# The order of a feed-forward kernel's opening: byte stores on other queues, earlier fetches, and a written order of loads and stores in its first stage

## The chip, the cores and the metric

The kernel runs on one core of a Trainium2 chip. The time is that of the device for one execution, in microseconds; before the change the median of three runs was 2055.12 us (2054.68 to 2055.93).

Five engines work side by side, each through its own instructions in order: TensorE (PE: matrix products and transposes into PSUM), VectorE (DVE), ScalarE (ACT), GpSimd (POOL) and SyncE (SP, which here only issues DMAs). ACT and POOL can issue DMAs too. Engines wait for each other by semaphores. An instruction that waits holds back all that stand behind it on its engine.

## The reference

The input is u, 2 x 1024 rows of 1024 values. Three blocks are added to it in turn: half a feed-forward block, a state-space convolution (S4), and half the same feed-forward block again.

```python
x = L0_attn_u
x = x + 0.5 * ffn(layernorm(x))
x = x + s4(layernorm(x))
x = x + 0.5 * ffn(layernorm(x))

def ffn(x):
    Wg, Wu, Wd = dequant(gate), dequant(up), dequant(down)
    h = silu(x @ Wg) * (x @ Wu)
    return h @ Wd

# W[k, n] = scales[k // 128, n] * (w4[k, n] - (z4[k // 128, n] + 1))
```

The weights are 4-bit numbers, eight to a 32-bit word, with a scale and a zero point for every 128 rows of a column. Gate and up have 1024 rows and 2752 columns, down has 2752 rows and 1024 columns.

## The kernel before, in words

The 2048 rows are taken in four blocks of 512. Each passes the feed-forward block twice, so there are eight jobs (j = 0 to 7). Each job has a gate and up stage and then a down stage.

**The gate and up stage** (`gate_up`) runs over 64 steps. A step is a wave w (three, and in the last three waves two, column blocks of 128 of gate and as many of up) and a group g of 128 rows of the weights, g = 0 to 7. In each step every unit (one block of gate or up; a wave of three has six) gets two products of 128 x 128 by 128 x 512: the normalized input is split into xTh (about the upper part of each number) and xTl (the rest), and both are multiplied by the same whole-number weights (L803). A unit has one PSUM bank. After both products of a group the bank is multiplied in place by the ratio of two groups' scales (`scaled`: L766 on ACT or L770 on DVE), so that the sums of all groups add up in the bank. I call that an eviction, though the values stay in the bank. Units of gate go to ACT, units of up to DVE, with exceptions for the second unit of a wave (L816): in job 0 it goes to ACT at g = 0 and g = 4. After the last group, ACT takes the Silu of gate (L831), DVE multiplies with up (L834), and POOL splits the result in two (L836, L838). Only then are the two banks free for the next wave. There are eight banks, and six are held by a wave of three.

**The weights.** For each step a tile of bytes is loaded by SP from `w_q[w]` in HBM four steps ahead (`load_bytes`, L727), and three steps ahead it is cast to 32-bit numbers (`make_weights`), by POOL (L743), or by ACT in job 0 where s mod 8 is 1, 2 or 5 (L741). The bytes in `w_q` are made in job 0 itself. Wave by wave, the packed words are fetched (`fetch`, L556), the unpacked zero points are fetched from `z_dram`, spread over 16 rows each (`fetch_zeros`, L563), DVE turns the words into two sets of bytes (`split` with `signed_bytes`: mask L617, add L619, sign L621, for the even and the odd nibbles), POOL copies out each of the eight nibble positions (`dequantize`, L650), and SP stores them to `w_q` (L651). So in job 0 the load for a wave's step has to wait for all eight stores of that wave. `first_weights` says at which step each piece is placed: words and zeros of wave w + 1 three steps into wave w's own schedule, and so on.

**The opening** (`start`) does the same for wave 0 by `first_split`: its words come from SP and ACT, DVE makes the bytes, POOL copies out nibbles 1, 3, 5, 7, 4 and 6 (L601) and ACT 0 and 2 (L599). Each copy is stored twice: 16 of its 128 rows into the first weight tile in SBUF (L602, SP), and all of it to `w_q[0]` (L604; by SP for 0 and 2, by POOL for the others). Meanwhile x is loaded and its mean and variance are found (`first_moments`: DVE for rows 0 and 2, ACT for 1 and 3), the deviation's inverse r is found by an integer guess (L203 to L209) and three refinements (L224 to L228), and the rows are normalized (`first_rows`, by DVE for even t in the first half, else by ACT). PE transposes them in chunks of 128 columns (`first_turn`, L1751); ACT copies the result to xTh (L1753) and DVE subtracts for xTl (L1754). `keep_warm` gives PE transposes whose results nobody uses. The zero points are unpacked by DVE (L355, L364) and stored to `z_dram` by SP (L383). The scales of wave 0 are loaded and turned, copied by DVE (L426), inverted and made into ratios (L392 to L432). Chunks 0 and 1 are turned in `start`, chunks 2 to 7 in steps 0 to 5.

**What sets the order.** The code places pieces at steps as hooks: `at(up, s, f)` runs f before the matmuls of step s, and at s + 0.5 after half of them. But the tile framework may reorder instructions of an engine by its own estimate of times. `in_order_of_writing(f, engines)` (and `pinned`, which wraps it) forbids that: each instruction that f writes for one of these engines is bound to come after the one written before it. `STARTING` is ACT, DVE and SP; `start` is pinned on these and PE.

## Time and profile before

| what | value |
|---|---|
| median of 3 runs | 2055.12 us (2054.68 to 2055.93) |
| the profiled execution | 2054.89 us |
| its span in the trace | 2053.0 us |
| granted TensorE clock, mean | 0.998 |
| first matmul with weights (L803) | 22.46 us |
| end of job 0's gate and up stage | about 200 us |
| PE busy | 2007.7 us (98%) |
| DMA, share of 16 engines, main queue | 35.0% |

How to read it: times are counted from the start of the span. A row of a timeline gives start, length, engine, line of the code, operation, and the tiles (output <- input); "x3" joins three like instructions, and brackets give the idle time before and who ended it. An engine's name with q (SPq, ACTq) is its queue of DMA issues. In a view of stretches, each engine has its busy time and the number of instructions in it (an instruction across an edge counts on both sides), and the last three columns are the granted clock of PE, the share of the DMA engines in use and GB/s; columns of engines without such instructions are left out. PEld is the load of weights into PE, which runs beside the matmuls. Matmul lengths are modelled, so gaps and starts say more than busy time. A wait is put down to whoever came last by the profile.

### The profile page before, as it was taken

How to read it: one execution, taken by the hardware profiler on the slowest of the kernel's cores; microseconds unless marked ns; L12 is line 12 of the kernel's file. 1: busy time of each engine (PE TensorE's matmuls, PEld its weight loads, DVE VectorE, ACT ScalarE, POOL GpSimd, SP SyncE). 2: the span in 40 equal slices, each digit the busy share in tenths (PEclk: the TensorE clock that was granted, in tenths of full speed). 3: DMA queues.
4: the chain of work that ended last, by engine and by line, in shares of the span. 5: the costliest groups of instructions: out<-in, count | busy, mean ns of one | idle time of the engine just before them, and what ended most of it. 6: DMA issues, size and time to landing. Idle time of an engine off the chain costs nothing.

```text
span 2053.0 us, 29946 instructions
## 1 busy us (share of the span) xinstructions
PE 2007.7 (98%) x9204; PEld 1371.8 (67%) x9204; DVE 1653.2 (81%) x2836; ACT 1409.5 (69%) x2208; POOL 1353.4 (66%) x1742
## 2 busy tenths in 40 slices
PE   6999999999999999999999999999999999999998
PEld 4555775577766678665876578667686576866576
DVE  8888878867888787878778777887878878777776
ACT  6777787747675476777767777664776647767775
POOL 5867768657865478755976568753686646965542
PEclk9999999999999999999999999999999999999999
DMA  4434332243623227411462126333163331661113
GB/s 142 124 89 146 115 87 78 60 78 99 166 79 85 88 49 187 146 32 35 121 183 81 31 51 164 87 83 90 40 158 104 71 92 41 156 189 42 34 35 102
DMA packets 346887, 197.15 MB, mean 96 GB/s; under 512 B 168069, under 2 KB 324590, under 8 KB 346718
## 3 DMA queue, kind: packets, MB, share of 16 engines
q1 hardware_dynamic: 345414, 192.74, 35.0%
q8 instruction: 75, 1.23, 0.2%
q10 hardware_dynamic: 1016, 1.82, 0.2%
q14 instruction: 94, 0.77, 0.1%
q0 software_dynamic: 288, 0.59, 0.1%
HBM read 127.52 MB, written 48.57 MB: 86 GB/s over the span
## 4 chain that ended last, share of the span: by engine, by line
PE 91%; DVE 3%; POOL 2%; DMA 1%; issue 1%; ACT 1%; SPq 0%; ACTq 0%; POOLq 0%; DVEq 0%
PE pg L803 56%; PE po L877 30%; PE pc L1245 3%; PE pb L1245 1%; DVE pg L770 1%; DMA b<-wq 1%; POOL hh L836 0%; POOL w_up L743 0%; ACT pg L766 0%; POOL hl L838 0%; DMA x<-in_L_attn_u_dram 0%; POOL q L650 0%; POOL sums L1239 0%; DMA st<-sz 0%; DVE hf L834 0%
## 5 line engine op out<-in xcount | busy, mean ns | idle before, releaser
L766 ACT ACTIVATE pg<-pg,rat 128x512 f32<-128x512 f32 x1270 | 801.6, 661 | 398.6 <-PE pg L803 394.7
L770 DVE TENSOR_TENSOR pg<-pg,rat 128x512 f32<-128x512 f32 x1138 | 755.1, 692 | 142.9 <-PE pg L803 135.2
L803 PE MATMUL pg<-xTh,w_up 128*128 128x512 f32 x2752 | 851.1, 437 | 2.8 <-DVE pg L770 1.9
L803 PE MATMUL pg<-xTl,w_up 128*128 128x512 f16 x2752 | 715.8, 382 | 9.2 <-DVE pg L770 3.8
L743 POOL CAST w_up<-b 128x768 fp32r<-128x768 int8 (+2 forms) x490 | 376.4, 775 | 396.8 <-PE pg L803 286.6
L803 PEld LDWEIGHTS pg<-xTh,w_up 128*128 128x128 f32 x2752 | 519.2, 189 | 170.5 <-issue 10.4
L766 ACT ACTIVATE po<-po,ratd 128x512 f32<-128x512 f32 x669 | 438.0, 662 | 144.0 <-PE po L877 143.1
L877 PE MATMUL po<-hl,w_down 128*128 128x512 f32 x1344 | 526.4, 393 | 2.5 <-DVE po L770 1.3
L877 PE MATMUL po<-hh,w_down 128*128 128x512 f32 x1344 | 521.4, 390 | 0.0
L770 DVE TENSOR_TENSOR po<-po,ratd 128x512 f32<-128x512 f32 x611 | 423.8, 696 | 112.0 <-PE po L877 111.3
L803 PEld LDWEIGHTS <-w_up 128*128 128x128 bf16 x2752 | 226.8, 98 | 347.8 <-issue 164.3
L743 POOL CAST w_down<-bd 128x512 fp32r<-128x512 int8 x352 | 218.6, 625 | 152.0 <-PE po L877 75.9
L877 PEld LDWEIGHTS po<-hl,w_down 128*128 128x128 f32 x1344 | 251.9, 188 | 64.9 <-DVE po L770 4.4
L877 PEld LDWEIGHTS po<-hh,w_down 128*128 128x128 f32 x1344 | 252.4, 188 | 50.8
L838 POOL TENSOR_TENSOR hl<-hf,hh 128x512 fp32r<-128x512 f32 x168 | 218.7, 1302 | 7.1
L836 POOL CAST hh<-hf 128x512 fp32r<-128x512 f32 x168 | 108.0, 643 | 76.2 <-DVE hf L834 46.2
L834 DVE SCALAR_TENSOR_TENSOR hf<-pg,rat,g 128x512 f32<-128x512 f32 x168 | 120.9, 746 | 40.7 <-ACT g L831 30.6
L831 ACT ACTIVATE g<-pg,rat 128x512 f32<-128x512 f32 x168 | 110.1, 687 | 34.9 <-PE pg L803 18.2
L930 POOL TENSOR_TENSOR x<-x,yr 128x512 f32<-128x512 f32 x52 | 67.0, 1288 | 0.0
L295 POOL TENSOR_TENSOR lo<-x,hi 128x512 f16<-128x512 f32 x48 | 62.5, 1301 | 0.0
L189 DVE BATCH_NORM_STATS2 stats<-x 128x6 f32<-128x512 f32 x88 | 59.9, 681 | 0.0
L293 POOL TENSOR_TENSOR mid<-hi,top 128x512 bf16<-128x512 f32 x48 | 56.2, 1171 | 0.0
(214 smaller groups left out, 1083.6 us busy)
## 6 DMA issues: line engine op xcount, KB each, us to landing
b<-wq SPq DMA_DIRECT2D x319, 96.0 KB
bd<-wdq SPq DMA_DIRECT2D x336, 64.0 KB
x<-in_L_attn_u_dram SPq DMA_DIRECT2D x30, 512.0 KB
yz<-y SPq DMA_DIRECT2D x56, 256.0 KB
yr<-yz SPq DMA_DIRECT2D x56, 256.0 KB
b<-wq SPq DMA_DIRECT2D x128, 64.0 KB
sz<-xn SPq DMA_DIRECT2D x16, 512.0 KB
st<-sz SPq DMA_DIRECT2D x64, 128.0 KB
```

The costliest lines, as they stand in the source:

```text
L295: nc.gpsimd.tensor_tensor(lo[:, own], n[:, own], hi[:, own].bitcast(F32), ALU.subtract)
L743: nc.gpsimd.tensor_copy(t, b)
L766: nc.scalar.activation(dst, src, AF.Copy, scale=sc)
L770: nc.vector.tensor_tensor(dst, src, sc.to_broadcast(list(dst.shape)), ALU.mult)
L803: nc.tensor.matmul(p, weights, (lo, hi)[k][:, g, :], start=(g == 0 and not done), stop=(g == GK - 1 and done), skip_group_check=True,)
L831: nc.scalar.activation(g, pg, AF.Silu, scale=rat[:, 2 * f, GK - 1 :])
L834: nc.vector.scalar_tensor_tensor(hf, pu, last, g, ALU.mult, ALU.mult)
L836: nc.gpsimd.tensor_copy(hi, hf)
L838: nc.gpsimd.tensor_tensor(lo, hf, hi.bitcast(F32), ALU.subtract)
L877: nc.tensor.matmul(ps[c], w[:, bass.ts(c, P)], part, start=(f == 0 and k == 0), stop=(f == NF - 1), skip_group_check=True,)
L930: nc.gpsimd.tensor_tensor(part, part, rows_back.pop((a, t)), ALU.add)
L1245: nc.tensor.matmul(dst, lhsT, rhs, start=start, stop=stop, skip_group_check=True)
```

## The change

- **Byte stores of wave 0.** `first_split` gets a function `keep`, so that storing to `w_q[0]` is separate from copying out. Nibbles 1, 3, 5, 7 are stored by SP, 4 and 6 by POOL after all its copies, 0 and 2 by ACT.
- **Wave 1's words** are fetched before the moments of x are taken, and no longer after all copies.
- **Zero points.** The eight unpacking instructions go between the moments and the guess; the last one follows the second group of rows; the store to `z_dram` and the fetch of wave 1's zeros are placed at step 0, pinned on SP. Wave 2's words and zeros follow at steps 1 and 2.
- **Scales of wave 0.** Turned after four warming transposes, copied by ACT instead of DVE; the inverse is written between xTh and xTl of chunk 0. The rows of scales for blocks 3 to 8 are loaded at step 1 instead of in `start`.
- **Rows and chunks.** The order of the row pieces in `start` changes; the second halves of rows 0 and 2 go from ACT to POOL; chunks 1 and 2 come in the middle of step 0, chunk 3 at step 1, chunk 4 in the middle of step 2; they are pinned on PE too, and chunks 2 and 3 on POOL. The second halves of rows 1 and 3 come at steps 0.5 and 1, pinned on ACT.
- **Matmuls and evictions.** In job 0 the matmuls of steps 0 to 5 are pinned on PE, step 0's evictions on ACT and DVE. In job 0 the second unit of a wave goes to ACT only at g = 4.
- **Loads and stores.** In job 0, `next_weights` is pinned on SP for steps below 52. `dequantize` no longer stores; `keep_bytes` does, at steps of its own, pinned on SP. The copies of wave 1 are all placed at step 3.
- **Within a split** both masks come first, then add and sign of each half.

The diff, cut to its core:

```diff
@@ -379,6 +379,7 @@
         yield from unpacked_zeros_in_pieces(tab, z, zi)
+        yield
         dst, seg = (zd_dram, SEGD) if which else (z_dram, SEG)
         nc.sync.dma_start(dst.rearrange("g (s n) -> (g s) n", s=seg), tab)
@@ -408,7 +409,10 @@
     def scales(k0, k1, rows):
-
+        for _ in scales_in_pieces(k0, k1, rows, nc.vector.tensor_copy):
+            pass
+
+    def scales_in_pieces(k0, k1, rows, copy):
...
-        nc.vector.tensor_copy(flat(s), ps[:, : (u1 - u0) * GK])
+        copy(flat(s), ps[:, : (u1 - u0) * GK])
+        yield
         inv = t2(f"inv_{k0}")[:, : (u1 - u0) * GK]
         inverse(inv, flat(s), k0)
@@ -600,10 +605,13 @@
             nc.sync.dma_start(first_tile[j:P:8], q[: P // 8])
-            queue = nc.sync if j in (0, 2) else nc.gpsimd
-            queue.dma_start(w_q[0].rearrange("(r j) n -> j r n", j=8)[j], q)
-
-        return rest, dequantize
+            bytes_of[j] = q
+
+        def keep(j, queue):
+            queue.dma_start(w_q[0].rearrange("(r j) n -> j r n", j=8)[j], bytes_of.pop(j))
+
+        bytes_of = {}
+        return rest, dequantize, keep
@@ -613,9 +621,10 @@
         for part, (n, shift) in zip((even, raw), shifts):
+            nc.vector.tensor_scalar(part, raw, n, NIBBLES, shift, ALU.bitwise_and)
+            yield
+        for part in (even, raw):
             both = part.bitcast(U16)
-            nc.vector.tensor_scalar(part, raw, n, NIBBLES, shift, ALU.bitwise_and)
-            yield
             nc.vector.tensor_tensor(both, both, z.bitcast(U16), ALU.add)
             yield
             nc.vector.tensor_scalar(both, both, 0x8080, None, ALU.bitwise_xor)
@@ -648,9 +657,14 @@
         nc.gpsimd.tensor_copy(q, packed[w][j % 2][:, j // 2, :])
-        nc.sync.dma_start(w_q[w].rearrange("(r j) n -> j r n", j=8)[j], q)
+        ready[w, j] = q
         if j == 7:
             packed.pop(w)
+
+    ready = {}
+
+    def keep_bytes(w, j):
+        nc.sync.dma_start(w_q[w].rearrange("(r j) n -> j r n", j=8)[j], ready.pop((w, j)))
@@ -688,14 +702,19 @@
         for w in range(1, len(WAVES)):
             s0 = (0, 4, 8 * w - 15)[min(w, 3) - 1]
-            steps = (0, 1, 2, 2, 3, 3) if w == 1 else range(6)
+            steps = (0.5, 1, 2, 2.5, 2.5, 3) if w == 1 else range(6)
             in_pieces(at, [(up, s0 + d) for d in steps], lambda w=w: split(w))
-            copies = {1: (2, 2, 3, 3, 3, 3, 3, 3), 2: (3, 3, 4, 4, 6, 6, 7, 7)}
+            copies = {1: (3,) * 8, 2: (3, 3, 4, 4, 6, 6, 7, 7)}
+            copies = copies.get(w, (3, 3, 4, 5, 6, 6, 7, 8))
+            stores = {1: (3,) * 8, 2: (4.5, 4.5, 5.5, 5.5, 7, 7, 7.5, 7.5)}
+            stores = stores.get(w, [d + 1.5 for d in copies])
             if 1 < w < len(WAVES) - 1:
                 both = lambda w=w: (fetch(w + 1), fetch_zeros(w + 1))
                 at(up, s0 + 3, lambda both=both: in_order_of_writing(both, ET.SP))
-            for k, d in zip((0, 2, 4, 6, 1, 3, 5, 7), copies.get(w, (3, 3, 4, 5, 6, 6, 7, 8))):
+            for k, d, o in zip((0, 2, 4, 6, 1, 3, 5, 7), copies, stores):
                 at(up, s0 + d, lambda w=w, k=k: dequantize(w, k))
+                store = lambda w=w, k=k: keep_bytes(w, k)
+                at(up, s0 + o, lambda store=store: in_order_of_writing(store, ET.SP))
@@ -773,7 +792,7 @@
         for s, (wi, g) in enumerate(STEPS):
-            w = next_weights()
+            w = in_order_of_writing(next_weights, *[ET.SP] * (j == 0 and s < 52))
             for hook in hooks.get(s, ()):
                 hook()
@@ -800,7 +819,7 @@
-                nc.tensor.matmul(
...
+                in_order_of_writing(product, *[ET.PE] * (j == 0 and s < 6))
                 if not done:
                     continue
                 if g < GK - 1:
                     on_act = unit % 2 == 0
                     if unit == 2 * fs[0] + 1:
-                        on_act = (j == 0 and g % 4 == 0) or (j == 1 and g % 2 == 0)
+                        on_act = (j == 0 and g == 4) or (j == 1 and g % 2 == 0)
                         on_act = on_act or (j in (3, 4) and 24 < s < 33)
                     if unit == 2 * WIDE:
                         on_act = g % 2 == 0
-                    scaled(on_act, p, p, rat[:, unit, g : g + 1])
+                    rescale = lambda: scaled(on_act, p, p, rat[:, unit, g : g + 1])
+                    in_order_of_writing(rescale, *STARTING[:2] * (j == s == 0))
@@ -1612,20 +1633,24 @@
             if j == 0:
-                rows = {3: srow_next}
-                for first_use, s, k0, k1 in ((5, 0, 3, 9), (14, 6, 9, 15), (30, 11, 15, WIDE)):
-                    if k0 > 3:
-                        load = lambda k0=k0, k1=k1: rows.update({k0: scale_rows(k0, k1)})
-                        at(up, s, lambda load=load: in_order_of_writing(load, ET.SP))
+                rows = {}
+                for s, f in ((0, lambda: next(points, None)), (0, lambda: fetch_zeros(1)), (1, lambda: fetch(2)), (2, lambda: fetch_zeros(2))):
+                    at(up, s, pinned(f, ET.SP))
+                for first_use, s, k0, k1 in ((5, 1, 3, 9), (14, 6, 9, 15), (30, 11, 15, WIDE)):
+                    load = lambda k0=k0, k1=k1: rows.update({k0: scale_rows(k0, k1)})
+                    at(up, s, lambda load=load: in_order_of_writing(load, ET.SP))
                     at(up, first_use, lambda k0=k0, k1=k1: scales(k0, k1, rows.pop(k0)))
                 at(up, 36, lambda: rows.update(down=scale_rows_down()))
...
-                for c in range(2, NC):
+                for c in range(1, NC):
                     more = lambda c=c: rows_by_chunk(c)
-                    at(up, c - 2, lambda more=more: in_order_of_writing(more, *STARTING))
+                    at(up, {1: 0.5, 2: 0.5, 4: 2.5}.get(c, c - 2), pinned(more, *STARTING, ET.PE, *[ET.Pool] * (1 < c < 4)))
+                for i, t in enumerate((1, 3)):
+                    more = lambda t=t: first_rows(t, 512, HID)
+                    at(up, 0.5 + i / 2, pinned(more, ET.Activation))
@@ -1732,12 +1757,13 @@
-        if t % 2 or half:
+        if t % 2:
             nc.scalar.activation(n, src, AF.Identity, bias=first["bias"][:, t : t + 1], scale=r)
         else:
-            nc.vector.tensor_scalar(n, src, m, r, ALU.subtract, ALU.mult)
-
-    def first_turn(c):
+            e = nc.gpsimd if half else nc.vector
+            e.tensor_scalar(n, src, m, r, ALU.subtract, ALU.mult)
+
+    def first_turn(c, between=lambda: None):
...
         if c != 5:
             nc.scalar.copy(hi, ps)
+            between()
             nc.vector.tensor_tensor(lo, ps, hi.bitcast(F32), ALU.subtract)
     def rows_by_chunk(c):
-        if c < 4:
+        if 1 < c < 4:
             first_rows(2 * c - 4, 512, HID)
         first_turn(c)
@@ -1781,38 +1808,41 @@
-        rest, dequantize_first = first_split(zq)
-        for j in (1, 3, 5, 7):
-            dequantize_first(j)
-        mv, scratch = first_moments({0: rest, 2: lambda: None})
+        rest, dequantize_first, keep_first = first_split(zq)
+        for pair in ((1, 3), (5, 7)):
+            for j in pair:
+                dequantize_first(j)
+            for j in pair:
+                keep_first(j, nc.sync)
+        fetch(1)
+        points = zero_points_in_pieces(0, zeros)
+        mv, scratch = first_moments({0: rest, 2: lambda: [next(points) for _ in range(8)]})
         for j in (4, 6, 0, 2):
             dequantize_first(j)
-        fetch(1)
-        rows_next = scale_rows(3, 9)
-        keep_warm(22, scratch)
+        for j in (4, 6):
+            keep_first(j, nc.gpsimd)
+        keep_warm(4, scratch)
+        first_scales = scales_in_pieces(0, 3, srow, nc.scalar.copy)
+        next(first_scales)
+        for j in (0, 2):
+            keep_first(j, nc.scalar)
+        keep_warm(12, scratch)
         bias = small.tile([P, NT], F32, tag="bias", name="bias")
         r = deviations(0, 1, LIFT)
         nc.vector.scalar_tensor_tensor(bias, mv[:, :, 0], -1.0, r, ALU.mult, ALU.mult)
         first["bias"] = bias
         for t in range(NT):
             first_rows(t, 0, P)
-        zero_points(0, zeros)
-        for t in (0, 2):
+        for t in (0, 1):
             first_rows(t, P, 512)
-        first_turn(0)
-        for t in (1, 3):
+        first_turn(0, lambda: next(first_scales, None))
+        for t in (2, 3):
             first_rows(t, P, 512)
+        next(points)
         keep_warm(6)
-        scales(0, 3, srow)
-        first_turn(1)
-        for t in (1, 3):
-            first_rows(t, 512, HID)
-        fetch_zeros(1)
-        fetch(2)
-        fetch_zeros(2)
-        return rows_next, zeros_down
-
-    srow_next, zeros_down = in_order_of_writing(start, *STARTING, ET.PE)
+        return points, zeros_down
+
+    points, zeros_down = in_order_of_writing(start, *STARTING, ET.PE)
```

More of the change, by code (lines that the diff above doesn't have):

```diff
@@ L615, in signed_bytes @@
         for part, (n, shift) in zip((even, raw), shifts):
-            both = part.bitcast(U16)
             nc.vector.tensor_scalar(part, raw, n, NIBBLES, shift, ALU.bitwise_and)
             yield
+        for part in (even, raw):
+            both = part.bitcast(U16)
             nc.vector.tensor_tensor(both, both, z.bitcast(U16), ALU.add)
@@ L802, in gate_up @@
                     weights = weights.bitcast(BF16).rearrange("p (n k) -> p k n", k=2)[:, 1, :]
-                nc.tensor.matmul(
+                product = lambda: nc.tensor.matmul(
                     p,
```

## The prediction

> **What bounds the kernel now.** I read the page first, then TensorE's (PE's) matmuls by stretch, then what PE waits for, then the timeline of the first 25 us and the chain of waits where it stalls longest.
>
> The page's first part and its clock row:
>
> ```profile
> PE 2007.7 (98%) x9204; PEld 1371.8 (67%) x9204; DVE 1653.2 (81%) x2836; ACT 1409.5 (69%) x2208; POOL 1353.4 (66%) x1742
> ...
> PEclk9999999999999999999999999999999999999999
> ```
>
> PE is the bound, so a microsecond by which its first matmul comes earlier, or a gap that closes, should come off the end. The change touches only the start and the first gate and up stage (j = 0). That stage in three stretches, matmuls of L803 alone (length, busy and count):
>
> ```profile
> 22.40:83.05 60.65, 50.91 (x204) 26.80 (x205) 0.97 0.44 127
> 83.05:147.90 64.85, 62.99 (x278) 37.47 (x277) 1.00 0.31 90
> ```
>
> PE's steady pitch is read from a stretch without gaps: 144 instructions in 32.35 us (83.05 to 115.40), 0.225 us each. At it the first 204 need 45.9 us; 24 transposes of x after the first matmul (0.11 us each in the timeline) add 2.6 and 15 of scales 1.0. So 49.5 us would do where 60.65 passed: 11.1 us are lost, after 22.46 us before the first matmul. From 83.05 on hardly anything is lost (DVE waits of 2.7 us in all up to 205). Who held PE, 0 to 205 us (total, times, longest):
>
> ```profile
> PE pg L803 <- DVE pg L770: 3.5, 9, 0.8
> PE pg L803 <- ACT g L831: 3.1, 1, 3.1
> PE pg L803 <- POOL w_up L743: 1.7, 2, 1.2
> PE pt L1751 <- DVE xn L1738: 1.4, 2, 0.8
> PE pt L1751 <- DVE xTl L1754: 1.2, 1, 1.2
> ```
>
> The opening, from the timeline (start, length):
>
> ```profile
> 14.19 2.14 DVE L207 TENSOR_SCALAR half<-ve 128x4 int32<-128x4 int32 x1
> ...
> 14.71 1.60 POOL L601 COPY q<-even_w 128x768 int8<-128x768 int8 x2
> ...
> 18.18 0.50 SPq L602 DMA_DIRECT2D b<-q  x1
> ...
> 20.21 1.00 POOL L743 CAST w_up<-b 128x768 fp32r<-128x768 int8 x1 [2.90 <-DMA b<-q]
> ```
>
> Two chains meet at the first matmul: the bytes (last store into the first weight tile issued by 18.68, landed 1.53 later, cast to 21.2), and the normalization (r known at 18.50 because one 128x4 instruction took 2.14 us, then rows, transposes, xTh and xTl to 22.4). The longest stall, from the chain of waits:
>
> ```profile
> 70.80 0.30 SPq L563
> ...
> 72.27 4.19 DMA b<-wq
> ...
> 77.28 0.83 ACT w_up L741
> 78.10 0.59 ACT g L831
> ...
> 78.74 11.32 PE pg L803 x42
> ```
>
> SP issued the loads of the fifth wave's words and zeros (L563) ahead of a weight tile's load, which took 4.19 us to land beside them. ACT stood 3.35 us in front of the cast of that tile, and the Silus that free PE's banks stood behind it. PE was idle from 75.65 to 78.74. It pays twice:
>
> ```profile
> 78.80:82.30 3.50, 3.50 (x9) 1.99 (x9) 2.13 (x3) 2.83 (x5) 3.08 (x5) 0.51 0.33 111
> ```
>
> After the gap the granted clock was 0.51 for 3.5 us, so 1.75 more was lost.
>
> **Part by part.** *The start, bytes.* Six stores of wave 0 went from POOL (0.54 to 0.73 us each, between its casts) and two from SP. Now SP takes j = 1, 3, 5, 7, POOL 4 and 6 after all its casts, ACT 0 and 2. SP's queue, from its rows (tile store 0.50, byte store 0.58, fetch 0.43): two tile stores after the casts at 10.12 and 10.9, to 11.40; two byte stores to 12.55; again two and two to 14.70; wave 1's fetch, two DMAs, to 15.55; four tile stores to 17.55, instead of 18.68. Landed 1.53 later, at 19.1; cast by 20.1. The Trainium skill speaks against moving stores (DMA: Bandwidth & Descriptors, Rules for kernel authors): spreading DMAs over SP, ACT and GpSimd brings no bandwidth, for all share the same engines, and saves the issuing engine's time only. The rows agree on the price, since the DMA share is 0.26 from 10 to 20 us. By the rule alone the edit is worth nothing on the wire; by the rows issue time is just what this chain is made of, so I count 1.1 us.
>
> *The start, normalization.* Eight zero-unpacking instructions (0.83 us) leave the place after the rows and go to 12.77, where DVE waits 0.92 us for ACT's squares; ztab (0.52) goes behind xTl. The casts of j = 4 and 6 no longer wait for POOL's stores (2 x 1.07 and 1.28 us between pairs), so the six end near 14.1 and not at 16.3. That matters for L207: such a 128x4 instruction takes 0.17 (L209), and it took 2.14, ending 0.03 after POOL's casts. The Trainium skill (SBUF — State Buffer, Who interferes with whom) says why: DVE's two-port forms and GpSimd share one port pair under an exclusive lock, and the later one blocks fully. By the row, L207 at 14.19 finds POOL done and r is ready at 16.5 (L209 ran its 0.17 under a POOL store). By the rule the unpacking, now beside POOL's casts, may itself block to 14.1 and push everything behind it: r at 17.75. Neither end is excluded; I take 17.3, gain 1.2. From r: rows 0.9 on ACT, a further row piece 0.66 (now ahead of xTh), xTh 0.59, xTl 0.68; on DVE the inverse of the scales (1.3, now between) is done by 19.8. So xTl is ready near 20.5, and the weights near 20.1: first matmul 20.5, gain 2.0 (0.6 to 2.6). The scale copy (0.25) and two stores (about 0.6 each) on ACT lie in its idle 3.43 us before the rows; warm-up falls from 22 to 16 transposes plus 3, and the clock is already full.
>
> *Steps 0 to 7.* Before, ACT did three half-row normalizations (2.23) before it evicted step 0's banks. Now two go to POOL, two come later, step 0's evictions are held in written order, and PE's first six steps too. POOL pays two 128x512 instructions: nearest rows, cast 0.62 and two-input subtract 1.29; it reads one tensor, so about 0.8 each, and they lie in the 5.94 us that POOL stood idle before 33.55. g = 0 of the second unit moves from ACT to DVE, +0.63 us (three in 1.88) per wave on DVE. By dependences, step 1 starts 3.7 us after step 0 (six matmuls 1.35, ACT two evictions and xTh 1.9 more, xTl), not 4.75. Later steps lose less to ACT and to the wait for a bank; DVE is 93% busy here (14.04 of 15.10 us, 36.5 to 51.6), which limits it. Of the 6.0 us lost outside the long stall I take half, 3.0 (from -1.5 to +5).
>
> *SP's fixed order.* Weight loads up to step 51 now stand before the same step's fetches and stores, and byte stores come 1 to 1.5 steps after their copies. Queued behind a waiting store are only later steps' loads, 4 steps (11 us) ahead of use. The tile that landed late would be issued as soon as wave 2's bytes are home, about 68, and not behind five other DMAs. The 3.5 us between matmuls and the 1.75 of clock should go: 5.0 with a small rest. Next late is the last byte store of wave 1: raw bytes from about 32, POOL then has 8 copies (6.6), chunk 5 (2.6) and a cast (0.8) and ends near 39.5; store, load and cast (1.9 + 2.4 + 0.8) give 44.7, while step 8 starts near 48. Cover about 3 us. Wave 1's zeros are written after ztab, near 23, and fetched by 26.5, while DVE needs them near 28.
>
> *Later waves.* DVE gets 0.63 us more in each of five waves, at 86% load (94.64 of 110 us from 90 to 200). ACT is relieved by as much just when it has three Silus. Between -3.3 and +1 I take -0.8, since DVE waits showed in the last four waves alone. The extra yields and the changed order within the split cost nothing: same instructions.
>
> **Sum.** 2.0 + 3.0 + 5.0 - 0.8 = 9.2 us. The profiled execution took 2054.89 (span 2053.0 and 1.9 around it): 2045.7. The median of 2055.12 is 0.23 above it: 2045.9, say 2046.
>
> **The rivals.**
> - *The stall moves on* (0.25): the long wait goes, but POOL's copies or DVE's evictions hold PE for several short ones, so the middle term is 0 and DVE costs 2: 2.0 + 5.0 - 2 = 5, 2050. For it: DVE's 93%, and POOL instructions drawn out to 1.55 us beside DVE's. Against: POOL idle 7.3 us for late weight bytes, which now come earlier.
> - *Only the start gains* (0.10): another dependence sets SP's order (wave 2's bytes are home at 68 anyway), and the tile still meets the fetches on the wire. 2.0, and 2053. Against: the chain shows SP's own issues directly ahead of the late load.
> - *Slower* (0.06): the order holds SP at the head. Eight stores of wave 1 stand at step 3 ahead of step 8's load. If POOL's last copy ends after 43 us rather than 39.5, each us is idle PE, and from about 3 us of idleness the clock halves as it did at 78.7. Five us plus 1.7 at step 8, and the same at step 16, is 13.4 against 9.2: 2059.
> - *The forecast* (0.59): 2046, own range 2042 to 2049.
>
> Within 0.2% (4.1 us) is about what a measurement of this kernel can't tell from no change. Faster by more takes the forecast and over nine tenths of the first rival, 0.83; same 0.11; slower 0.06. The range, 2042 to 2051.5, leaves out the slower case, most of the third, and the upper ends of start and steps together.
>
> **What would show it.** First matmul near 20.5 and L207 near 0.2 us; if L207 is still long or the unpacking takes over 1 us, the lock went the other way. The 204th matmul near 73 rather than 83. No ACT wait for b of over 1 us near 70, and clock 1.00 from 75 to 85. SP's loads ahead of the fetches; the last store of wave 1 near 40. DVE waits after 83 at most 4 us. I am wrong if PE still has a gap of 3 us before 85, or if the stage after 83 (116.8 us now) grows by more than 3.

## The result, and the profile after

The changed kernel took 2052.48 us (median of 22 runs, 2051.34 to 2056.78) against 2055.65 (22 runs) before: a ratio of 0.9986, interval 0.9979 to 0.9992. The gain is real, 3.2 us (1.6 to 4.3), a third of the 9.2 forecast, and the time lies above the range. The profiled execution has a span of 2050.5 us. Its page:

```profile
PE 2006.6 (98%) x9198; PEld 1371.1 (67%) x9198; DVE 1655.4 (81%) x2843; ACT 1403.3 (68%) x2199; POOL 1351.8 (66%) x1740
...
PEclk9999999999999999999999999999999999999999
```

The averages hardly move; what moved is seen when the products with weights are counted (12 in a step of waves 0 to 2) and the start of the n-th is compared, in us:

| product | before | after | difference | forecast for this stretch | measured |
|---|---|---|---|---|---|
| 1st | 22.46 | 20.69 | -1.77 | -2.0 | -1.77 |
| 181st (step 15) | 72.78 | 71.91 | -0.87 | -3.0 | +0.90 |
| 205th (step 17) | 83.07 | 79.65 | -3.42 | -5.0 | -2.55 |
| 688th (end of the stage) | 199.27 | 194.93 | -4.34 | +0.8 | -0.92 |

The sum at the 688th is 4.3, and the spans differ by 2.5; the rest of the program gives some back, and the difference of the medians, 3.2, lies between the two. The matmuls by stretch, as before (length, busy and count, clock):

```profile
20.60:79.60 59.00, 50.23 (x204) 1.00 0.44 125
79.60:144.45 64.85, 63.05 (x280) 1.00 0.33 94
```

The first stretch holds the same 204 products and is only 1.65 us shorter, about as much as the clock alone had cost (1.75); what the long stall and the start released was used up by other gaps. The second row was given the same length as before, so the length says nothing; counted by products, the 205th to the 481st took 64.51 us against 64.76, so VectorE's extra evictions cost nothing there. Who held PE from 0 to 205 us (total, times, longest):

```profile
PE pg L822 <- DVE pg L789: 6.1, 8, 1.5
PE pg L822 <- POOL w_up L762: 1.4, 1, 1.4
PE pg L822 <- ACT g L852: 1.3, 1, 1.3
```

The wait of 3.1 us for ScalarE's Silu became 1.3, and VectorE's evictions took its place: 6.1 us instead of 3.5. That is the rival "the stall moves on" (2050), worked further than it was priced.

The opening, from the timeline:

```profile
12.26 2.10 DVE L355 TENSOR_SCALAR zi<-zq 128x43 int32<-128x43 int32 x8
...
14.75 0.17 DVE L207 TENSOR_SCALAR half<-ve 128x4 int32<-128x4 int32 x1
...
15.53 2.40 SPq L607 DMA_DIRECT2D b<-q  x4
...
19.30 0.69 DVE L1781 TENSOR_TENSOR xTl<-pt,xTh 128x512 f16<-128x512 f32 x1
19.80 0.83 POOL L762 CAST w_up<-b 128x768 fp32r<-128x768 int8 x1 [4.50 <-DMA b<-q]
```

L207 is down from 2.14 to 0.17 us; GpSimd's copies of the bytes (L606) now end at 14.03, before it. The eight unpacking instructions took 2.10 instead of 0.83 beside those copies: two of them took 0.84 instead of 0.19 and ended 0.06 us after a copy each. What the Trainium skill (SBUF — State Buffer, Who interferes with whom) says of a shared port was paid there, on a smaller scale. The low part xTl was ready at 19.99 (forecast 20.5), so it is the bytes that set the first product: last store issued by 17.93 (forecast 17.55), cast done at 20.63 (20.1).

The place of the long stall, from the timeline (SyncE's loads at L746 and fetches at L561 and L568, ScalarE, and PE where it waited):

```profile
67.78 0.32 SPq L746 DMA_DIRECT2D b<-wq  x1
68.19 0.38 SPq L561 DMA_DIRECT2D raw<-_L_ffn_gate_qweight_dram  x1
68.63 0.42 SPq L561 DMA_DIRECT2D raw<-in_L_ffn_up_qweight_dram  x1
69.14 1.23 SPq L568 DMA_DIRECT2D z<-z_dram  x2
70.42 0.45 SPq L746 DMA_DIRECT2D b<-wq  x1
...
75.02 0.83 ACT L760 CAST w_up<-b 128x768 fp32r<-128x768 int8 x1 [2.46 <-DMA b<-wq]
75.76 0.68 ACT L852 ACTIVATE g<-pg,rat 128x512 f32<-128x512 f32 x1
...
76.49 0.38 PE L822 MATMUL pg<-xTl,w_up 128*128 128x512 f16 x1 [1.28 <-ACT g L852]
```

ScalarE at the same place in the kernel before:

```profile
76.54 1.56 ACT L741 CAST w_up<-b 128x768 fp32r<-128x768 int8 x2 [3.35 <-DMA b<-wq]
78.01 1.83 ACT L831 ACTIVATE g<-pg,rat 128x512 f32<-128x512 f32 x3
```

Step 17's tile (the load at 70.42) still stands behind the fifth wave's words and zeros, and is still late: ScalarE stood 2.46 us before its cast (3.35 before the change). Two things differ. The load is issued 1.85 us sooner than before (72.27), and its cast starts 1.52 us sooner. And the order on ScalarE behind it is another: before, both late casts (steps 17 and 18) stood ahead of the three Silus; now one Silu stands between the two casts, at 75.76, which is worth the 0.7 us of a cast. So the first Silu comes 2.25 us sooner, while PE runs out of work 0.4 us sooner (75.22 against 75.64). PE's gap is 1.28 us instead of 3.09, and the clock stays at 1.00.

### The profile page after: what moved, and what is told of

It is laid out like the page before. It is cut to its first block, busy times and chain, and to the rows that moved or that the text cites. A ratio compares the mean times of both kernels' runs of the same rounds, so it can differ in the third digit from the quotient of the medians.

```text
span 2050.5 us, 29905 instructions
## 1 busy us (share of the span) xinstructions
PE 2006.6 (98%) x9198; PEld 1371.1 (67%) x9198; DVE 1655.4 (81%) x2843; ACT 1403.3 (68%) x2199; POOL 1351.8 (66%) x1740
## 4 chain that ended last, share of the span: by engine, by line
PE 90%; DVE 3%; POOL 3%; DMA 1%; issue 1%; ACT 1%; SPq 1%; POOLq 0%; DVEq 0%; ACTq 0%
PE pg L822 55%; PE po L898 30%; PE pc L1266 3%; PE pb L1266 1%; DVE pg L789 1%; POOL q L659 1%; POOL hl L859 1%; DMA b<-wq 1%; POOL hh L857 0%; DMA wq<-q 0%; POOL w_up L762 0%; ACT pg L785 0%; DVE hf L855 0%; POOL sums L1260 0%; DVE po L789 0%
```

## The experiments

All are timed beside the kernel before on the same chip. Their ratios stand against 0.9986 (0.9979 to 0.9992) for the changed kernel. Each edit is made to the changed kernel, unless the kernel before is named.

### The parts undone one by one

**Half rows back on ScalarE** (`first_rows`):

```diff
-        if t % 2:
+        if t % 2 or half:
```

> The two half-row normalizations of steps 0 and 1 are done by ACT again (0.74 us each) and no longer by POOL (2.08 us each in the changed kernel's trace). Theory (POOL, slowed by these two, holds up the weight casts and wave 1's byte copies): wave 1's last byte store ends about 2 us earlier than 43.7, the 97th product starts about 1 us before 50.35, and the whole is 0.5 to 1.5 us faster than the changed kernel. Rival (DVE's evictions pace steps 0 to 7, POOL does not): within 0.4 us of it, or slower, because ACT holds up step 0's evictions again.

Ratio 0.9984 (0.9977 to 0.9991), the same, although each half row costs GpSimd far more than the 0.8 us of the forecast. The changed kernel's timeline has:

```profile
23.91 2.08 POOL L1764 TENSOR_SCALAR xn<-x,mv,r 128x512 f32<-128x512 f32 x1
```

So 2.6 us were mis-sized in the two rows, and they cost nothing in the end. The 97th product, expected about 1 us sooner than 50.35, came at 51.83, because this profile started late (21.58) with a halved clock. From the 13th to the 97th product it needed 24.60 us; the run with a later start (below), which leaves the rows on GpSimd, needed 24.48. So nothing shows that the rows took the middle term.

**The g = 0 eviction back on ScalarE**:

```diff
-(j == 0 and g == 4)
+(j == 0 and g % 4 == 0)
```

> Only the eviction of a wave's second unit at g = 0 goes back from DVE to ACT in job 0. Rival theory (the eviction that was put on DVE in each wave is what ate the start's gain, since PE's waits for DVE grew from 3.5 to 6.1 us): PE's waits for DVE up to 84 us fall by 1.5 to 2.5, and the whole is as much faster than the changed kernel. My theory: it is worth no more than 0.7 us either way, because ACT has the Silus at that point; the 97th product is within 0.5 us of 50.35.

Ratio 0.9987 (0.9981 to 0.9994), the same. The 181st product came 0.78 us earlier (71.13), the 205th 1.33 later (80.98): what VectorE gains in waves 0 and 1, ScalarE loses at the Silus, where PE waits 1.66 us and the clock halves. PE's waits for VectorE up to 84 us fell from 4.0 to 3.0 us only, less than the rival theory asked.

**Weight loads not pinned on SyncE**:

```diff
-            w = in_order_of_writing(next_weights, *[ET.SP] * (j == 0 and s < 52))
+            w = in_order_of_writing(next_weights, *[ET.SP] * (j == 0 and s < 0))
```

> Only the pinning of the weight loads on SP is taken away; stores keep their places. Theory (the written order is close to the order that stood there before, as far as the loads of steps 8 and 16 to 18 go): within 1 us of the changed kernel. Rival (the pinned loads are what saved the 3.4 us at the long stall): slower than the changed kernel by 2 us or more, with ACT's wait for b near 75 back at 3 us or more.

Ratio 1.0006 (0.9997 to 1.0014): the whole gain is gone. But SyncE issues the two loads at 67.82 and 70.48, within 0.06 us of 67.78 and 70.42. The timeline shows what changed with the pin:

```profile
75.29 0.83 ACT L760 CAST w_up<-b 128x768 fp32r<-128x768 int8 x1 [4.42 <-DMA b<-wq]
76.03 1.23 ACT L785 ACTIVATE pg<-pg,rat 128x512 f32<-128x512 f32 x2
76.74 0.57 PE L822 MATMUL pg<-xTl,w_up 128*128 128x512 f16 x1 [4.32 <-ACT pg L785]
```

ScalarE's cast now stands ahead of two evictions, PE waits 4.32 us for them, and the clock halves for 3.4 us. So at this place the pin did its work by moving the cast on another engine, which the framework orders by its estimates, and not by issuing the load sooner.

**The pin alone, in the kernel before** (the same line written into it):

> The kernel before with the weight loads of steps below 52 pinned on SP, nothing else of the change. It shifts the framework's estimate, and on ACT the first Silu of wave 1 now stands between the casts of steps 17 and 18 and not behind both, while the fetch still stands ahead of the load of step 17 on SP. Theory (ACT's place in the queue counts, not SP's order): the stall at 75.65 shortens by a cast and the clock stays full or nearly so, 1 to 3 us faster there; the start may lose up to 1 us, since zeros now stand ahead of the first loads on SP. Rival (SP's order): no change beyond 0.7 us at the stall.

Ratio 1.0039 (1.0025 to 1.0052), some 8 us slower (5 runs), where 1 to 3 us faster was expected. Zeros and words of the next waves, which the change moves away, stand ahead of the first loads: the 13th product comes at 33.96 instead of 27.21. A Silu does stand between the two late casts, as expected, but ScalarE waits 5.28 us for the first cast's bytes, and at 81.8 PE waits 4.55 us for that Silu. So the place on ScalarE alone does not save the stall; when the bytes come counts too. The pin is worth something only with the rest of the change. The direction of the rival "slower" was possible, by another mechanism than it named.

### The long stall

**The casts of ScalarE moved to other steps**:

```diff
-        if j == 0 and stage == "up" and s > 2 and s % GK in (1, 2, 5):
+        if j == 0 and stage == "up" and s > 2 and s % GK in (5, 6, 7):
```

> In job 0, ACT casts the weights of the steps with s mod 8 = 5, 6, 7 in place of 1, 2, 5; POOL casts the others. So no cast that waits for a wave's first bytes stands ahead of the previous wave's Silus on ACT. Theory (what PE pays at steps 8 and 16 is ACT's queue: a cast that waits for its bytes, with evictions and Silus behind it): ACT's wait for b near 75 goes, PE's longest gap between 70 and 85 falls under 0.7 us, the 205th product starts near 77.0 (79.65 in the changed kernel), the whole is 2 to 3 us faster than the changed kernel. Rival (the bytes themselves come too late for PE): the wait moves to POOL's casts of steps 17 and 18, PE waits for w_up, gain under 0.5 us.

The 205th product came at 76.55 us, 3.1 sooner, but the end not: 0.9990 (0.9982 to 0.9999). The next cast on ScalarE, with three evictions behind it, took over, and the clock was halved for 3.4 us from 83.2 on:

```profile
80.44 0.83 ACT L760 CAST w_up<-b 128x768 fp32r<-128x768 int8 x1 [3.19 <-POOL hh L857]
...
81.89 0.95 PE L822 MATMUL pg<-xTl,w_up 128*128 128x512 f16 x3 [2.48 <-ACT pg L785]
```

**The same edit in the kernel before:**

> The kernel before with that one edit alone. Theory: the long stall there (75.65 to 78.74, and the halved clock after it) goes without anything of the change, the 205th product starts near 78.5 instead of 83.07, the whole is 4 to 5 us faster than the kernel before, thus as fast as the changed kernel or faster. Rival (late bytes): under 1.5 us.

Ratio 0.9985 (0.9978 to 0.9992). This one line gains as much as the whole change, though less than the 4 to 5 us expected: the 3.09 us gap is gone, the 205th comes at 81.41 instead of 83.07, although a new gap of 2.03 us near 64 halves the clock for 3.4 us.

**Evictions to ScalarE besides** (the second unit's at g = 2 and 6 in steps 1 to 15 as well as at g = 4, on top of the moved casts):

> The changed kernel with the casts as in the kernel with late casts on ACT, and in steps 1 to 15 of job 0 the second unit's evictions at g = 2 and 6 on ACT as well as those at g = 4: four times 0.63 us less for DVE, four times 0.66 more for ACT. Theory (DVE, 21.50 of 21.56 us busy from the 97th to the 181st product, is what gave the start's gain back): the 181st product starts 1 to 2.5 us before that of the kernel with late casts alone, and the whole is as much faster than it. Rival (DVE is busy but not binding; POOL's copies are): within 0.5 us of it.

Ratio 1.0015 (1.0008 to 1.0021), slower. PE's waits for VectorE were 5.3 us, more than the 4.7 of the run with moved casts alone, and ScalarE's own evictions held PE for 5.2 instead of 3.6. The clock was halved three times, once of them at the start, which the edit does not touch. Shifting evictions between these two engines did not help here.

**All fetches from the fifth wave's on (wave 4, counted from 0) two steps later**:

```diff
-                at(up, s0 + 3, lambda both=both: in_order_of_writing(both, ET.SP))
+                at(up, s0 + (5 if w > 2 else 3), lambda both=both: in_order_of_writing(both, ET.SP))
```

> From wave 3's schedule on, the fetch of the next wave's words and zeros comes two steps later, so that on SP it stands behind the loads of steps 17 and 18 (and 25, 26 and so on) and not ahead of them. Theory (the rest of the long stall is the fetch that the change left ahead of the load of step 17, on SP's queue and on the wire): ACT's wait for b before 75.0 (2.46 us) falls under 0.6, the load lands in about 2 us and not 4.5, the 205th product starts about 2 us before 79.65, the whole is 1.5 to 2.5 us faster than the changed kernel. Rival (POOL's byte copies of wave 2, which end at 66 in both kernels, set the load): gain under 0.7 us.

Ratio 1.0006 (0.9999 to 1.0013). Step 17's load is in front now and the 205th product 0.77 us sooner (78.88), but at 95.3 PE waits 3.23 us for evictions behind a cast whose load came late, and the clock halves.

**The fifth wave's fetch alone** (`5 if w == 3 else 3`; the rest as it was):

> The changed kernel with the fetch of one wave's words and zeros, the fifth's, placed two steps later, so that the loads of steps 17 and 18 stand ahead of it on SyncE; the fetches of the later waves stay. It makes true what the forecast said of the change and what the trace of it doesn't show. Theory 1, the forecast's step was right but not carried out by the change: step 17's tile is issued near 68 and lands by 70.5, ScalarE waits for it at most 1.2 us, the 205th product comes near 78, no new wait near 97 as when all fetches moved, end 2050.8. Theory 2, the fifth wave's own chain is then late: a gap of over 1.5 us between 95 and 105 us, end within 1 us of 2052.5 or later.

It does what the forecast said of the change. SyncE issues both loads at 68.0 in one row, and ScalarE waits 0.99 us:

```profile
68.03 0.80 SPq L746 DMA_DIRECT2D b<-wq  x2
...
70.66 0.84 ACT L760 CAST w_up<-b 128x768 fp32r<-128x768 int8 x1 [0.99 <-DMA b<-wq]
```

The 205th came at 78.18 (78 expected), the gap of 1.28 us is gone. The end is not earlier: 0.9989 (0.9983 to 0.9996). A gap of 1.22 us opened at 95.0, and the 289th product is 0.49 us later than in the changed kernel.

**Only the casts of steps 17 and 18 to GpSimd** (`and s not in (17, 18)`):

> The changed kernel with the casts of steps 17 and 18 alone moved from ScalarE to GpSimd; the order of SyncE's DMAs is the same. Theory 1, the place of the cast ahead of the Silus on ScalarE is what is left of the long wait: PE's gap of 1.28 us at 76.5 goes, the 205th product comes near 77.2 us (79.65 in the changed kernel), and as ScalarE's later casts stay where they are, no new gap follows at 79 or 182 as with all casts moved; end 2050.2. Theory 2, the stall moves on whatever is moved: the gap is found again within 10 us, at GpSimd's cast or at the halves of h that GpSimd splits behind it, and the end is within 1 us of 2052.5.

The 205th at 77.05, as expected; the end 0.9986 (0.9980 to 0.9993), against expectation. The 2.6 us were given back in three gaps for evictions behind ScalarE's casts:

```profile
81.07 0.95 PE L822 MATMUL pg<-xTl,w_up 128*128 128x512 f16 x3 [1.17 <-ACT pg L785]
...
96.99 0.95 PE L822 MATMUL pg<-xTl,w_up 128*128 128x512 f16 x3 [1.09 <-ACT pg L785]
```

The third, of 0.76 us, lies at 92.

### What the stall moves to

The stretches of the run with the fifth wave's fetch alone around its new gap (PE, PEld, DVE, ACT, POOL busy and count, then clock, DMA share, GB/s):

```profile
85.00:92.50 7.50, 7.50 (x35) 4.47 (x34) 6.80 (x13) 6.28 (x11) 7.42 (x8) 1.00 0.37 111
92.50:100.00 7.50, 6.28 (x29) 3.70 (x27) 5.28 (x10) 5.08 (x8) 6.12 (x9) 1.00 0.46 134
```

GpSimd is busy for 7.42 of 7.50 us before the gap, with the byte copies (3.95 us for four), whose stores stand on SyncE ahead of the loads. Two runs, both with the one fetch later, tell place and work apart.

**Stores one step later, behind the loads**:

```diff
-            stores = stores.get(w, [d + 1.5 for d in copies])
+            stores = stores.get(w, [min(d + 2.5, 10) for d in copies])
```

> The changed kernel with the fifth wave's fetch two steps later, as in the run before it, and with the byte stores of waves 3 and later one step later as well, so that each weight load stands on SyncE ahead of the stores that wait for GpSimd's copies. Theory 1, the load behind a waiting store is the new wait: SyncE issues the loads near 93 us about 1.5 us earlier, the 1.22 us gap at 94.6 goes, the 205th product stays near 78.2 and the 289th comes near 97.4 (99.07 with the fetch alone, 98.58 in the changed kernel), end near 2051.2. Theory 2, GpSimd's copies set it, whatever the order of the DMAs: a gap of over 0.8 us between 90 and 105 us remains, the 289th within 0.6 of 98.6, the end within 1 us of 2052.8. Against theory 1 too: the last store of a wave is then only one step ahead of that wave's first load, which may make a new gap near 107.

A gap of 1.04 us remains at 93.1; ratio 0.9989 (0.9983 to 0.9996). The stores' place on the queue is not it.

**Half of GpSimd's copies of waves 3 and 4 left out** (in `dequantize`):

```diff
+        if w in (3, 4) and j in (2, 6, 3, 7):
+            q = ready_last[0]
+        else:
             q = qpool.tile(...)
             nc.gpsimd.tensor_copy(q, packed[w][j % 2][:, j // 2, :])
+        ready_last[0] = ready[w, j] = q
```

> The changed kernel with the fifth wave's fetch two steps later, and with every second of GpSimd's byte copies of waves 3 and 4 left out (the copy before it is stored twice, so half of the weights of these two waves are wrong numbers); eight copies of 0.83 to 1 us less on GpSimd between 67 and 100 us, about 7 us; the order of the DMAs and of ScalarE is the same. Theory 1, the stores' place behind GpSimd's copies or its load sets the pace: the gap of 1.22 us at 94.6 goes, the 181st product is unmoved at 72, the 205th near 77.8, the 289th near 97.2, end near 2051.0. Theory 2, ScalarE's or VectorE's own work or the DMA's landing sets it: a gap of over 0.8 us between 90 and 105 us remains and the end is within 1 us of 2052.8.

```profile
85.00:92.50 7.50, 7.02 (x32) 4.11 (x31) 7.23 (x12) 6.00 (x10) 5.71 (x6) 1.00 0.09 29
92.50:100.00 7.50, 7.50 (x35) 4.70 (x33) 6.65 (x12) 6.21 (x11) 4.28 (x6) 1.00 0.50 146
```

The gap is gone (PE 7.50 of 7.50 from 92.5 on; a small one of 0.48 us came at 87.1). This run starts 0.36 us later than the run with the fetch alone, yet its 289th product comes 0.95 us sooner (98.12). Its ratio, 0.9974 (0.9963 to 0.9984; 8 runs), is the best of all runs. So GpSimd's copying is what the gain of an earlier 205th product runs into. By which way is not separated: with fewer copies SyncE also fetches the next wave's words 4.5 us sooner (80.58 against 85.10), so the DMA share just before the gap falls from 0.37 to 0.09.

### The start and the middle

**A later start** (`keep_warm(24)` for the last `keep_warm(6)`):

> The changed kernel with 18 more warming transposes on PE before its first product (18 times 0.11 us, 2.0 us), nothing else changed. Theory 1, what the start gains is passed on to the end: first product near 22.7 us, the 49th near 38.7, the 181st near 73.9, the end 2.0 us later, 2054.5. Theory 2, the start's gain is swallowed because VectorE, which is 95% busy from 25 to 72 us, sets the pace of waves 0 to 2: first product near 22.7, the 49th at most 0.9 us later than in the changed kernel (37.6), the 181st within 0.5 of 71.9, the end within 0.7 of 2052.5.

The delay was smaller than meant: PE was idle before its first product anyway, so that came only 0.51 us later (21.20). Of that, 0.25 was left at the 37th product and 0.01 at the 49th (36.67 against 36.66); ratio 0.9988 (0.9982 to 0.9995). Half a microsecond at the start is swallowed within four steps. In the run with rows on ScalarE a delay of 2.07 us at the 49th product was still 1.77 at the 688th, in a profile with a halved clock at the start, so for larger delays this stays open.

**Less work for VectorE** (zero points and sign left out in waves 1 and 2):

```diff
-        for part in (even, raw):
+        for part in (even, raw) if key not in (1, 2) else ():
```

> The changed kernel in which the splits of waves 1 and 2 leave out the addition of the zero points and the flip of the sign, so the weights of these two waves are wrong numbers; VectorE has eight instructions less, four of about 1.05 us and four of about 0.70, 7.0 us in all, all before the 181st product. Theory 1, VectorE sets the pace of waves 0 to 2 and keeps the forecast's middle term from arriving: the 181st product 3 to 5 us earlier, near 68 (71.91 in the changed kernel), PE's waits for VectorE's evictions from 0 to 205 us down from 6.1 to about 3, the end near 2048.5. Theory 2, the banks, ScalarE or the bytes through memory set it: the 181st within 1 us of 71.9 and the end within 1 us of 2052.5. As wave 2's bytes come home earlier too, an earlier 205th product by itself is no evidence; the 49th to the 181st are.

Its first product waited 2.3 us for weights (21.95), and the clock was halved for 6.8 us from 20.8 on. From the 49th product (38.03) to the 169th (67.97) it needed 29.94 us, the changed kernel 32.54 (36.66 to 69.20). First this run, then the changed kernel:

```profile
38.03:67.97 29.94, 28.88 (x139) 17.45 (x136) 27.38 (x45) 22.79 (x37) 24.48 (x28) 1.00 0.40 118
36.66:69.20 32.54, 29.72 (x132) 16.40 (x130) 31.29 (x47) 22.95 (x38) 27.05 (x29) 1.00 0.34 101
```

VectorE is busy for 3.9 us less in this stretch (27.38 against 31.29; the rest of the 7.0 us spared lies before it), and 2.6 us of that arrive at PE. The late start does not explain it: the run with rows on ScalarE, 2.07 us late at the 49th product, needed 32.43. PE's waits for VectorE fell from 6.1 to 3.3. Then ScalarE stood before a late cast again:

```profile
71.23 0.83 ACT L760 CAST w_up<-b 128x768 fp32r<-128x768 int8 x1 [4.21 <-DMA b<-wq]
...
72.67 1.22 PE L822 MATMUL pg<-xTh,w_up 128*128 128x512 f32 x2 [2.96 <-ACT pg L785]
```

The 205th came at 82.23. Ratio 0.9981 (0.9973 to 0.9990), some 1 us better than the changed kernel, less than the intervals can tell. The 181st product, expected near 68, came at 74.99; this stall, with the clock halved from 72.0 on, and the late start together kept it.

## Why the prediction was wrong, point by point

- **The start** was right in its mechanism: 1.77 us of 2.0, with the lock priced between its two ends (r ready at 17.1, forecast 17.3). That the number fits so well is partly luck: the bytes came 0.5 us later than forecast and xTl 0.5 sooner, so the limit was the bytes, not xTl.
- **Steps 0 to 7**: the step that failed is "Of the 6.0 us lost outside the long stall I take half, 3.0". The stretch from the 1st to the 181st product became 0.9 us longer. The forecast named the limit itself ("DVE is 93% busy here") and then did not use it as one. The loss begins at once: from the 13th product to the 49th (steps 1 to 3) the changed kernel needs 11.86 us instead of 10.27. First before, then after (columns as in the stretches above):

```profile
27.21:37.48 10.27, 9.78 (x49) 6.00 (x47) 7.89 (x13) 9.19 (x17) 3.75 (x6) 1.00 0.41 112
24.80:36.66 11.86, 10.53 (x56) 6.59 (x54) 11.14 (x19) 8.65 (x15) 8.37 (x8) 1.00 0.52 139
```

  VectorE has 11.14 us of work here instead of 7.89, and PE's 1.3 us of idleness are waits for its evictions (0.75 of the 1.59 us is other work of PE that now lies in this stretch). From the 49th product to the 169th nothing is gained: 32.54 us against 32.56. The last part, from the 97th to the 181st, before and after:

```profile
51.65:72.78 21.13, 20.37 (x93) 10.90 (x92) 20.90 (x31) 14.85 (x25) 20.53 (x21) 1.00 0.42 125
50.35:71.91 21.56, 20.39 (x91) 11.36 (x91) 21.50 (x32) 14.87 (x26) 21.27 (x23) 1.00 0.38 110
```

  VectorE is busy for 21.50 of 21.56 us and GpSimd for 21.27; that the stretch was full could have been read before the change, at 20.90 of 21.13. Relieving ScalarE (14.87) could not help here: with its casts at other steps the 97th to the 169th product took 18.82 us, against 18.85. With less work for VectorE they took 16.81. With the eviction alone moved back the 181st product came 0.78 us sooner, and that was lost again at the Silus. VectorE is not the only limit of the steps before: from the 49th to the 97th product the run with moved casts needed 12.50 us, the changed kernel 13.69.
- **Half rows on GpSimd**: "so about 0.8 each" was 2.08, further off than either row it was taken from (0.62 and 1.29). No cost came of it.
- **SP's fixed order**: the step that failed is "would be issued as soon as wave 2's bytes are home, about 68, and not behind five other DMAs". It came at 70.42, 1.85 us sooner than before but behind the same four fetches; of the five DMAs only a store was gone from ahead of it. The written order itself has the fetch at step 12 and the load of step 17's tile at step 13; pinning keeps that. Of the 5.0 us, 1.75 of clock and 1.8 of the gap came nonetheless, about 1.1 of the gap because the cast came sooner and 0.7 by its changed place on ScalarE, and about 1 was lost between the 181st and the 205th product otherwise (0.35 of it waiting for VectorE's hf). The forecast never asked whether the order on ScalarE would change.
- **That closing the stall pays at the end** failed too. When the step was carried out (that fetch alone) the 205th product came 1.5 us sooner and the end did not. By the runs that follow it the next limit lies some 17 us behind, with GpSimd's copies for the next wave.
- **Later waves**: a loss of 0.8 us was forecast; from the 205th product to the 688th the profile is 0.92 us shorter instead.
- **Small errors of the working**: after the first matmul the trace has 20 transposes and 12 scale products before 83 us, not 24 and 15, so about 0.6 us more was lost than the 11.1; and PE stood 3.1 us before the Silus, not 3.5. Neither decides anything.
- **The rivals**: "the stall moves on" had the mechanism and 2050; it took the long wait as gone, which was half true. "Only the start gains" (2053) is nearest in time and wrong in cause, since half of the start's gain was lost again by step 15, and the larger part of what the stage gained (2.55 of 4.34 us) came at the stall.
- **The signs of being wrong**: neither of the two that were named came. No gap of 3 us was left before 85 us, and the stage after 83 did not grow. What told of the failure was among the signs of being right: the 204th product near 79 us and not near 73, and a wait of 2.46 us on ScalarE where at most 1 was to be left.

What stays open: how much of the start's 1.8 us reaches the end. Of the 4.3 us that the profile had gained at the end of the stage, 3.55 are left at the last product of the last down stage. From there to the end it took 12.1 us after the change and 11.1 before; over the 16 profiles this last piece lies between 10.7 and 12.2 us, so that 1 us is within its variation. Where the other 0.8 went in the jobs between was not looked into.

## What to carry to other kernels

A wait taken away was worth here only what lay between it and the next full engine: read the busy time of every engine in that very stretch, and if one has 21.5 of 21.6 us, count nothing for relieving another. A cast that waited for its bytes cost by when they came and by what stood behind it on its engine: with a wait of 2.46 us and one Silu next it cost PE 1.28 us, with 4.42 us and two evictions next 4.32. So look up its place there, also when an edit names only another queue, for a framework may reorder it. And where an order is pinned as written, read the written order first: it can hold the very sequence that was to be undone.

## What the runs showed of the hardware

- **The clock.** From the first warming transposes to 205 us the 16 profiles have 14 idle stretches of PE of 1.66 us or more (the longest 4.55), and the clock was halved in a window of 3.41 or 6.83 us around or right after each. After gaps of 1.0 to 1.64 us alone it was not; one of the windows (pin alone, at 29.9) began after two of these, 1.20 and 1.43 us within 3 us, and before the longer gap that it overlaps. One window of 3.41 us at half speed costs about 1.7 us of PE. The run with the g = 0 eviction back, with a gap of 1.66 us ending at 77.1, shows it:

```profile
77.40:80.80 3.40, 3.40 (x10) 0.50 0.48 145
```

  The Trainium skill (TensorE: Matmul & The Clock Gate, Part 1) has the same window, 3413 ns, but puts the halving after an idle window of about 3.4 us. By that rule only the gaps of 4.32 and 4.55 us could have been punished; here 1.66 sufficed.
- **GpSimd's tensor_scalar** on 128x512 numbers with two operands per row took 2.08 us, against 0.62 for a cast and 1.29 for a subtraction of two tensors of that size.
